# An attention and expert block on one core: the shared up weights of the tail fetched once, its first rows fetched early

## Chip, core and metric

The kernel runs on one core of one Trainium2 chip. The metric is the device time of one execution in microseconds, as the median of several runs. The profile is one further execution, recorded by the hardware profiler; its times are counted from the start of its span.

The engines are named as in the profile: PE (TensorE, matmuls; PEld its weight loads), DVE (VectorE), ACT (ScalarE), POOL (GpSimd), SP (SyncE, which here only issues transfers). "SPq", "ACTq" and "POOLq" are the queues of these engines where they issue a DMA.

## The reference

Eight sequences of 512 tokens with 512 features go through an attention block and a block of experts, each between two layer norms and with a residual. All is in float32.

```python
x = L0_attn_x                                   # 8 x 512 x 512
x = x + layernorm(attention(layernorm(x)))      # 16 heads, latent projections, rope scores
h = layernorm(x)
scores = sigmoid(h @ router_weight.T)           # 16 experts, 2 chosen per token, in groups
routed = sum over the 2 chosen: weight * relu2(h @ w_up[e]) @ w_down[e]     # 512 -> 256 -> 512
shared = relu2(h @ shared_up) @ shared_down                                 # 512 -> 1024 -> 512
x = x + layernorm(routed + shared)
```

`relu2` is the square of the ReLU. The shared part is computed for every token, the routed part only for the two experts of each token.

## The kernel before

There are four stages.

1. **Attention, with a side list.** A loop runs over the eight batches and 16 steps per batch. Beside the scores of a batch stand the closing work of the batch before (output projection, norm, router, scatter of its rows to `table`, sorted by expert) and, as fill, the shared part of earlier batches. `shared_list` (L641) makes that fill: per half batch (256 tokens, `a` = 0, 1) eight up chunks and four down pieces. The shared part is done here for all but the last `LATE = 2` batches, and its rows are stored to `s_rows` in DRAM. The rows after attention are stored to `x_rows` (L439).
2. **plan()** (L653) works out which tile of 128 routed rows belongs to which expert.
3. **routed()** (L728) runs over `NTILES` = 79 tiles of 128 rows: `fetch_rows` (L738) loads rows from `table`, `fetch_weights` (L743) loads one expert's up and down weights (512 KB each) into one of three sets if the expert has changed, `turn`, `up` and `down` compute, and ACT stores each result to `y_rows` (L789). In the loop at L797 tile j is computed, then SP issues the rows of tile j + 3 and the weights of tile j + 2.
4. **The tail** (L963 to L987) does the shared part of the last two batches and completes all 32 token tiles. `prepare` (L811) takes a slot of the pool `end`, loads the tile's `x_rows` and, for an early tile, its `s_rows` (256 KB each, on SP), and lets POOL gather the tile's two routed rows from `y_rows` (two indirect DMAs of 128 rows, L817). `complete` (L827) adds the parts on DVE (L830, L834), takes the norm's statistics (L213 to L217, L839), scales on ACT (L842), adds the residual on POOL (L843), and puts the store to `out` (L847) on a list. The list is emptied in the next `complete`.

The 24 tiles of the first six batches are early tiles: their shared rows come from `s_rows`. The eight tiles of the last two batches are late: their shared part comes straight from PSUM. The list `items` (L966 to L978) puts one early tile behind every two up chunks and one behind each late tile. So each half of a late batch completes eight tiles, in the order early, early, early, early, late, early, late, early; with four halves that makes 32.

In the tail the program's order is kept on PE and SP as written. DVE, ACT and POOL get theirs from a scheduler, and each works in order. SP's queue is one list: a store that waits for POOL's addition holds back all loads and weight fetches behind it. `LEAD = 6` tiles are prepared ahead, then tile n + 6 when tile n is completed. With `SLOTS = 10` slots a load of tile n waits until tile n - 10 is stored.

The up weights of the shared part (512 x 1024, 2 MB) come in pieces of 256 columns (512 KB) with two buffers. `load_wsu` (L590) is called by the first chunk of each piece and fetches that piece and the next:

```python
        if (b, a, i) not in wsu_ and b < B:
            wsu = sh.tile([P, NK, INTER], F32, tag="wsu", name=f"wsu_{b}_{a}_{i}", bufs=2)
            cols = shared_up[:, i * P : i * P + INTER]
            nc.sync.dma_start(wsu, cols.rearrange("(c p) i -> p c i", p=P))
```

A half batch uses four pieces, the tail 16. `shared_up_chunk` (L597) runs four matmuls per chunk (L609), then ReLU on ACT (L616) and the square on DVE (L617). `shared_down_tile` (L619) runs the down product (L624), 16 matmuls for one tile of 128 tokens in two pieces.

Of the kernel before, what the change touches and what calls it, by code (L numbers as in the profile page):

```python
# [11 lines left out]
F32 = mybir.dt.float32  # L12
# [5 lines left out]
P = 128  # L18
# [20 lines left out]
def sandwich_kernel(  # L39
# [28 lines left out]
    nc = tc.nc  # L68

    B, S, D = x.shape  # L70
    NE, _, INTER = w_up.shape
    HID = shared_up.shape[1]
    NT = S // P
    NK = D // P
    NI = INTER // P
    NH = HID // P
# [10 lines left out]
    ps_s = ctx.enter_context(tc.tile_pool(name="ps_s", bufs=2, space=PSUM))  # L87
    ps_o = ctx.enter_context(tc.tile_pool(name="ps_o", bufs=4, space=PSUM))
    dram = ctx.enter_context(tc.tile_pool(name="dram", bufs=1, space=bass.MemoryType.DRAM))
    until_tail = ExitStack()  # L90
    sb = until_tail.enter_context(tc.tile_pool(name="sb", bufs=1))
    until_routed = ExitStack()
    at = until_routed.enter_context(tc.tile_pool(name="at", bufs=1))

# [2 lines left out]
    NTILES = (TOP_K * T) // P + NE - 1  # L97
# [6 lines left out]
    def load_rows(src, b, name):  # L104
        t = sh.tile([P, NT, D], F32, tag="x", name=f"{name}_{b}", bufs=2)
        for i in range(NT):
            nc.sync.dma_start(t[:, i, :], src[b, i * P : (i + 1) * P, :])
        return t
# [304 lines left out]
    ao, xT, sc_, comb_, chosen_, slot_ = {}, {}, {}, {}, {}, {}  # L413

    def project_out(b, i):
        if i == 0:
            ao[b] = sb.tile([P, NT, D], F32, tag="ao", name=f"ao_{b}")
            res[b] = load_rows(x, b, "res")
        ps = ps_o.tile([P, D], F32, tag="o", name=f"ps_ao_{b}_{i}")
        for c in range(NK):  # L420
            nc.tensor.matmul(  # L421
                ps,
                lhsT=ctxs[b, c][:, i * P : (i + 1) * P],
                rhs=wo[:, c, :],
                start=(c == 0),
                stop=(c == NK - 1),
            )
        nc.vector.tensor_tensor(ao[b][:, i, :], ps, bo, ALU.add)
# [159 lines left out]
    hT, wsu_, ysum = {}, {}, {}  # L588

    def load_wsu(b, a, i):  # L590
        if (b, a, i) not in wsu_ and b < B:
            wsu = sh.tile([P, NK, INTER], F32, tag="wsu", name=f"wsu_{b}_{a}_{i}", bufs=2)
            cols = shared_up[:, i * P : i * P + INTER]
            nc.sync.dma_start(wsu, cols.rearrange("(c p) i -> p c i", p=P))
            wsu_[b, a, i] = wsu

    def shared_up_chunk(b, a, i, late):  # L597

        if i % NI == 0:
            load_wsu(b, a, i)  # L600
            load_wsu(b + (a and i + NI == NH), a ^ (i + NI == NH), (i + NI) % NH)
        if i == 0:
            hT[b] = sh.tile([P, NH, HALF], F32, tag="hT", name=f"hT_{b}_{a}")
        if late:
            ps = ps_s.tile([P, 2, S], F32, tag="s", name=f"h_{b}_{a}_{i}")[:, 0, :]
        else:
            ps = ps_o.tile([P, S], F32, tag="o", name=f"h_{b}_{a}_{i}")
        for k in range(NK):
            nc.tensor.matmul(  # L609
                ps[:, 0:HALF],  # L610
                lhsT=wsu_[b, a, i - i % NI][:, k, (i % NI) * P : (i % NI + 1) * P],
                rhs=xT[b][:, k, a * HALF : (a + 1) * HALF],
                start=(k == 0),
                stop=(k == NK - 1),
            )
        nc.scalar.activation(hT[b][:, i, :], ps[:, 0:HALF], AF.Relu)  # L616
        nc.vector.tensor_tensor(hT[b][:, i, :], hT[b][:, i, :], hT[b][:, i, :], ALU.mult)  # L617
# [21 lines left out]
    UP, DOWN = 1.72, 3.43  # L639

    def shared_list(b, finish, late=False):  # L641
        got = []
        for a in range(2):
            got += [(UP, lambda a=a, i=i: shared_up_chunk(b, a, i, late)) for i in range(NH)]
            got += [
                (DOWN, lambda a=a, t=t, i=i: shared_down_tile(b, a, t, i, finish))
                for t in range(NT // 2)
                for i in range(2)
            ]
        return got  # L650
# [77 lines left out]
    def routed(rt, lists):  # L728
# [14 lines left out]
        def fetch_weights(j):  # L743
            e = nc.sync.value_load(lists[0:1, 1, j : j + 1], min_val=0, max_val=NE - 1)
            load = nc.sync.value_load(lists[0:1, 2, j : j + 1], min_val=0, max_val=1)
            wu, wd = sets[j % NBUF]
            nc.sync.dma_start(
                wu, w_up[bass.ds(e, 1)].rearrange("o (c p) i -> p (o c) i", p=P), cond=load
            )
            nc.sync.dma_start(  # L750
                wd, w_down[bass.ds(e, 1)].rearrange("o (c p) d -> p (o c) d", p=P), cond=load
            )
# [44 lines left out]
        for j in range(NTILES + 1):  # L797
            if j + 1 < NTILES:
                turn(j + 1)
            if j < NTILES:  # L800
                up(j)
            if j > 0:
                down(j - 1)
            if j + AHEAD < NTILES:
                fetch_rows(j + AHEAD)
            if j + NBUF - 1 < NTILES:
                fetch_weights(j + NBUF - 1)

    def prepare(c, with_shared):  # L811
        t = end.tile([P, 4, D], F32, tag="end", name=f"end_{c}", bufs=SLOTS)
        nc.sync.dma_start(t[:, 0, :], x_rows[c * P : (c + 1) * P, :])
        if with_shared:
            nc.sync.dma_start(t[:, 1, :], s_rows[c * P : (c + 1) * P, :])
        for j in range(TOP_K):
            nc.gpsimd.indirect_dma_start(  # L817
                out=t[:, 2 + j, :],
                out_offset=None,
                in_=y_rows[:, :],  # L820
                in_offset=bass.IndirectOffsetOnAxis(ap=back[:, c, j : j + 1], axis=0),
            )
        return t

    SLOTS, LEAD = 10, 6

    def complete(c, t, shared=None):  # L827

        acc = t[:, 1, :]
        nc.vector.scalar_tensor_tensor(  # L830
            acc, t[:, 2, :], weight[:, c, 0:1], acc if shared is None else shared,
            ALU.mult, ALU.add,
        )
        nc.vector.scalar_tensor_tensor(  # L834
            acc, t[:, 3, :], weight[:, c, 1:2], acc, ALU.mult, ALU.add
        )
        mv, rstd = norm_stats([acc], f"y{c}")
        off = small.tile([P, 1], F32, tag="off", name=f"off_{c}")
        nc.vector.scalar_tensor_tensor(  # L839
            off, mv[:, 0, 0:1], -1.0, rstd, ALU.mult, ALU.mult  # L840
        )
        nc.scalar.activation(acc, acc, AF.Identity, bias=off, scale=rstd)  # L842
        nc.gpsimd.tensor_tensor(acc, acc, t[:, 0, :], ALU.add)  # L843
        while stores:
            stores.pop()()
        b, i = divmod(c, NT)
        stores.append(lambda: nc.sync.dma_start(out[b, i * P : (i + 1) * P, :], acc))  # L847

    stores = []


    LATE = 2
# [103 lines left out]
            f()  # L956
    until_routed.close()
    lists = plan()
    rt = until_tail.enter_context(tc.tile_pool(name="rt", bufs=1))
    with tc.manual_schedule(engines={mybir.EngineType.PE, mybir.EngineType.SP}):  # L960
        routed(rt, lists)
    until_tail.close()
    end = ctx.enter_context(tc.tile_pool(name="end", bufs=1))  # L963
    with tc.manual_schedule(engines={mybir.EngineType.PE, mybir.EngineType.SP}):

        early, items, ups, downs = iter(range((B - LATE) * NT)), [], 0, 0  # L966
        for b in range(B - LATE, B):
            late = iter(range(b * NT, (b + 1) * NT))
            for cost, f in shared_list(b, lambda ps, c: complete(c, ready.pop(c), ps), True):
                ups += cost == UP  # L970
                downs += cost == DOWN
                done = cost == DOWN and downs % 2 == 0
                items.append((f, next(late) if done else None))
                if done or cost == UP and ups % 2 == 0:
                    c = next(early, None)
                    if c is not None:
                        items.append((lambda c=c: complete(c, ready.pop(c)), c))
        items += [(lambda c=c: complete(c, ready.pop(c)), c) for c in early]  # L978
        order = [c for _, c in items if c is not None]
        ready = {}  # L980
        for f, c in [(None, None)] * LEAD + items:
            if f is not None:
                f()
            if (f is None or c is not None) and order:
                n = order.pop(0)
                ready[n] = prepare(n, n < (B - LATE) * NT)
        stores.pop()()  # L987


# [35 lines left out]
```

## Time and profile before

| what | value |
|---|---|
| three runs, median (lowest to highest) | 1939.24 us (1935.95 to 1941.33) |
| profiled execution, whole | 1946.77 us |
| profiled execution, span | 1945.1 us |
| mean granted clock of TensorE in it | 0.942 |
| busy: PE / DVE / ACT / POOL | 1726.6 / 1033.1 / 893.3 / 577.7 us |
| last routed product on PE (L780) begins | 1741.84 us |
| first and last gather on POOL (L817) begin | 1751.9 and 1908.0 us |
| last addition on POOL (L843) begins | 1940.5 us |
| transfers from 1735 to 1945 us | 48.91 MB |
| the same, by kind | 32 x_rows, 24 s_rows, 64 gathers, 32 stores (256 KB each), 15 up-weight pieces (512 KB each) |

The page gives an engine's busy time as a mean over the whole span. The tail is only a tenth of it, so it has to be read from the views that can be cut to a stretch of time: the timeline of one engine, and the busy times by window. In a line of a timeline the first number is the start, the second the duration, both in us; the bracket at the end gives the idle time before it and what ended that. "PEclk" is the share of TensorE's full clock that was granted, "DMA share" the mean busy share of the core's 16 DMA engines; small overlaps can take it a little above 1.

### The profile page before, as it was taken

How to read it: one execution, taken by the hardware profiler on the slowest of the kernel's cores; microseconds unless marked ns; L12 is line 12 of the kernel's file. 1: busy time of each engine (PE TensorE's matmuls, PEld its weight loads, DVE VectorE, ACT ScalarE, POOL GpSimd, SP SyncE). 2: the span in 40 equal slices, each digit the busy share in tenths (PEclk: the TensorE clock that was granted, in tenths of full speed). 3: DMA queues.
4: the chain of work that ended last, by engine and by line, in shares of the span. 5: the costliest groups of instructions: out<-in, count | busy, mean ns of one | idle time of the engine just before them, and what ended most of it. 6: DMA issues, size and time to landing. Idle time of an engine off the chain costs nothing. (4 is left out here: it accounts for less than half of the span.)

```text
span 1945.1 us, 27230 instructions
## 1 busy us (share of the span) xinstructions
PE 1726.6 (89%) x8968; PEld 1044.0 (54%) x8968; DVE 1033.1 (53%) x2695; ACT 893.3 (46%) x1977; POOL 577.7 (30%) x714
## 2 busy tenths in 40 slices
PE   7898999999999999999999989889689999996665
PEld 3444645555555545554655544445366777764443
DVE  4667745664665475446745665754522222225674
ACT  4866654654555555455545656751022222221222
POOL 1433332342324232423422353451100000006563
PEclk9999999999989998999999899889889999997787
DMA  6001111130112111211310110012456465578774
GB/s 199 1 23 44 63 58 44 55 109 33 45 54 93 49 50 39 82 49 55 105 36 23 55 66 1 22 44 70 179 184 233 131 207 180 196 266 283 261 267 153
DMA packets 125901, 199.62 MB, mean 103 GB/s; under 512 B 14145, under 2 KB 60225, under 8 KB 125761
## 3 DMA queue, kind: packets, MB, share of 16 engines
q1 hardware_dynamic: 102992, 141.50, 21.6%
q0 software_dynamic: 10240, 33.56, 4.6%
q10 hardware_dynamic: 12528, 22.81, 3.7%
q8 instruction: 73, 1.20, 0.2%
q14 instruction: 68, 0.55, 0.1%
HBM read 190.50 MB, written 65.01 MB: 131 GB/s over the span
## 5 line engine op out<-in xcount | busy, mean ns | idle before, releaser
L389 POOL TENSOR_SCALAR p<-p,rden 128x512 f32<-128x512 f32 x512 | 362.3, 726 | 788.6 <-DVE rden L387 480.7
L355 ACT ACTIVATE p<-p,nmax 128x512 f32<-128x512 f32 x512 | 363.8, 712 | 168.9 <-DVE nmax L345 161.6
L345 DVE CUSTOM_DVE_ANT_0 p<-s,rope 128x512 f32<-128x512 f32 x512 | 326.2, 686 | 93.1 <-PE s L333 69.0
L375 PEld LDWEIGHTS pt<-ident,p 128*128 128x128 f32 x2048 | 237.3, 146 | 183.7 <-issue 132.7
L609 PE MATMUL h<-xT,wsu 128*128 128x256 f32 x1024 | 251.0, 405 | 79.4 <-DMA wsu<-in_L_ffn_shared_up_dram 49.3
L375 PE MATMUL pt<-ident,p 128*128 128x128 f32 x2048 | 287.8, 285 | 25.4 <-DVE pT L378 9.1
L378 DVE COPY pT<-pt 128x512 f32<-128x512 f32 x256 | 175.1, 686 | 203.9 <-PE pt L375 197.7
L609 PEld LDWEIGHTS h<-xT,wsu 128*128 128x128 f32 x1024 | 206.2, 205 | 125.9 <-issue 50.8
L624 PE MATMUL y<-wsd,hT 128*128 128x512 f32 x512 | 228.5, 597 | 3.5 <-DVE pT L378 3.5
L380 ACT COPY pT<-pt 128x512 f32<-128x512 f32 x256 | 146.3, 576 | 112.2 <-PE pt L375 111.6
L817 POOL DMA_INDIRECT end<-y_rows,back x64 | 66.0, 1031 | 372.3 <-DMA end<-x_rows 354.3
L765 PE MATMUL hg<-xgT,set_up 128*128 128x128 f32 x1264 | 158.5, 280 | 13.3 <-DMA set_up<-in_L_ffn_w_up_dram 12.5
L333 PE MATMUL s<-k,q 32*128 32x512 f32 x1024 | 162.0, 671 | 1.9 <-DVE nmax L345 1.8
L624 PEld LDWEIGHTS y<-wsd,hT 128*128 128x128 f32 x512 | 96.6, 192 | 120.6 <-issue 111.0
L765 PEld LDWEIGHTS hg<-xgT,set_up 128*128 128x128 f32 x1264 | 150.8, 196 | 15.9 <-issue 11.8
L402 PE MATMUL o<-pT,v 128*32 128x512 f32 x1024 | 139.9, 625 | 18.7 <-DVE pT L378 17.9
L780 PE MATMUL yg<-set_down,hgT 128*128 128x512 f32 x316 | 149.7, 597 | 0.0
L774 DVE TENSOR_TENSOR hgT<-hgT 128x256 f32<-128x256 f32 x79 | 33.6, 426 | 186.4 <-ACT hgT L773 186.4
L617 DVE TENSOR_TENSOR hT<-hT 128x256 f32<-128x256 f32 x128 | 60.8, 477 | 122.4 <-ACT hT L616 117.3
L759 ACT COPY xgT<-pt_g 128x512 f32<-128x512 f32 x79 | 46.3, 586 | 161.8 <-PE pt_g L757 161.7
L616 ACT ACTIVATE hT<-h 128x256 f32<-128x256 f32 x128 | 48.5, 382 | 155.7 <-PE h L609 146.6
L421 PE MATMUL ps_ao<-wo,ctx 128*128 128x512 f32 x256 | 112.5, 593 | 0.0
(163 smaller groups left out, 1837.1 us busy)
## 6 DMA issues: line engine op xcount, KB each, us to landing
set_up<-in_L_ffn_w_up_dram SPq DMA_DIRECT2D x79, 512.0 KB
set_down<-in_L_ffn_w_down_dram SPq DMA_DIRECT2D x79, 512.0 KB
wsu<-in_L_ffn_shared_up_dram SPq DMA_DIRECT2D x64, 512.0 KB
xg<-table SPq DMA_DIRECT2D x79, 256.0 KB
y_rows<-ysb ACTq DMA_DIRECT2D x79, 256.0 KB
x<-in_L_attn_x_dram SPq DMA_DIRECT2D x32, 256.0 KB
res<-in_L_attn_x_dram SPq DMA_DIRECT2D x32, 256.0 KB
x_rows<-res SPq DMA_DIRECT2D x32, 256.0 KB
```

Of the source, the lines that this page charges most:

```text
L333: nc.tensor.matmul(tiles[-1][:, h % 2, :], lhsT=q[r0 : r0 + HEAD_DIM, qt * P : (qt + 1) * P], rhs=k[r0 : r0 + HEAD_DIM, :], start=True, st ...
L345: nc.vector.tensor_tensor_reduce(out=pr[:, h, :], in0=tiles[h // 2][:, h % 2, :], in1=rope[b, qt], scale=-1.0, scalar=3.0e38, op0=ALU.add, ...
L355: nc.scalar.activation(pr[:, h, :], pr[:, h, :], AF.Exp, bias=nmax[:, h : h + 1], scale=-1.0, accum_out=den[:, h : h + 1],)
L375: nc.tensor.transpose(pt[:, c, :], pr[:, h, c * P : (c + 1) * P], ident)
L378: nc.vector.tensor_copy(to, pt)
L380: nc.scalar.copy(to, pt)
L389: nc.gpsimd.tensor_scalar(pr[:, h, :], pr[:, h, :], rden[:, h : h + 1], 1.0, ALU.mult, ALU.mult)
L402: nc.tensor.matmul(ps[r0 : r0 + HEAD_DIM, :], lhsT=vs[b][:, c, col : col + HEAD_DIM], rhs=pT[:, h, c, :], start=(c == 0), stop=(c == NT - 1),)
L609: nc.tensor.matmul(ps[:, 0:HALF], lhsT=wsu_[b, a, i - i % NI][:, k, (i % NI) * P : (i % NI + 1) * P], rhs=xT[b][:, k, a * HALF : (a + 1) * ...
L624: nc.tensor.matmul(ysum[c], lhsT=hT[b][:, i, t * P : (t + 1) * P], rhs=wsd[:, i, :], start=(i == 0), stop=(i == NH - 1),)
L765: nc.tensor.matmul(ph[:, 0, i * P : (i + 1) * P], lhsT=sets[j % NBUF][0][:, k, i * P : (i + 1) * P], rhs=xgT[j][:, k, :], start=(k == 0), ...
L780: nc.tensor.matmul(py, lhsT=hg[j][:, i * P : (i + 1) * P], rhs=sets[j % NBUF][1][:, i, :], start=(i == 0), stop=(i == NI - 1),)
```

## The change

- The up weights of the late batches are no longer fetched in pieces. A tile `wsu_all` of 2 MB holds all of `shared_up`; it is fetched once, from inside `routed()`, behind the weights fetched in iteration j = 39. Its pool `late` is taken behind attention, in the space that attention's tiles leave.
- `prepare` is split into `load_end` (row loads on SP) and `gather_end` (gathers on POOL). The loads of the first `EARLY = 4` tiles stand at the end of the routed stage; their slots lie in the pool `late`.
- There are nine slots for ten (four in `late`, five in `end`), the lead is five tiles for six, and a store is issued when two tiles more have been completed (`LAG = 2`), not one.
- `ao` moves from the pool `sb` to the pool `at`, which ends before `plan()`; `sb` stays to the end.

```diff
-    until_tail = ExitStack()
-    sb = until_tail.enter_context(tc.tile_pool(name="sb", bufs=1))
+    sb = ctx.enter_context(tc.tile_pool(name="sb", bufs=1))
...
-            ao[b] = sb.tile([P, NT, D], F32, tag="ao", name=f"ao_{b}")
+            ao[b] = at.tile([P, NT, D], F32, tag="ao", name=f"ao_{b}")
...
-        if (b, a, i) not in wsu_ and b < B:
+        if (b, a, i) not in wsu_ and b < B - LATE:
...
-        if i % NI == 0:
-            load_wsu(b, a, i)
-            load_wsu(b + (a and i + NI == NH), a ^ (i + NI == NH), (i + NI) % NH)
+        if late:
+            wsu = wsu_all[:, :, i * P : (i + 1) * P]
+        else:
+            if i % NI == 0:
+                load_wsu(b, a, i)
+                load_wsu(b + (a and i + NI == NH), a ^ (i + NI == NH), (i + NI) % NH)
+            wsu = wsu_[b, a, i - i % NI][:, :, (i % NI) * P : (i % NI + 1) * P]
...
-                lhsT=wsu_[b, a, i - i % NI][:, k, (i % NI) * P : (i % NI + 1) * P],
+                lhsT=wsu[:, k, :],
...
+            if j == NTILES // 2:
+                nc.sync.dma_start(wsu_all, shared_up.rearrange("(c p) n -> p c n", p=P))
...
-    def prepare(c, with_shared):
-        t = end.tile([P, 4, D], F32, tag="end", name=f"end_{c}", bufs=SLOTS)
+    SLOTS, EARLY, LEAD, LAG = 9, 4, 5, 2
...
+    def load_end(n, c, with_shared):
+
+        pool, k = (late, EARLY) if n % SLOTS < EARLY else (end, SLOTS - EARLY)
+        t = pool.tile([P, 4, D], F32, tag="end", name=f"end_{c}", bufs=k)
         nc.sync.dma_start(t[:, 0, :], x_rows[c * P : (c + 1) * P, :])
         if with_shared:
             nc.sync.dma_start(t[:, 1, :], s_rows[c * P : (c + 1) * P, :])
+        return t
+
+    def gather_end(c, t):
         for j in range(TOP_K):
...
-    SLOTS, LEAD = 10, 6
...
-        while stores:
-            stores.pop()()
+        while len(stores) > LAG - 1:
+            stores.pop(0)()
...
+    late = ctx.enter_context(tc.tile_pool(name="late", bufs=1))
+    wsu_all = late.tile([P, NK, HID], F32, name="wsu_all")
+    until_tail = ExitStack()
     rt = until_tail.enter_context(tc.tile_pool(name="rt", bufs=1))
     with tc.manual_schedule(engines={mybir.EngineType.PE, mybir.EngineType.SP}):
         routed(rt, lists)
+        for n, c in enumerate(order[:EARLY]):
+            ready[c] = load_end(n, c, c < (B - LATE) * NT)
     until_tail.close()
...
-            if (f is None or c is not None) and order:
-                n = order.pop(0)
-                ready[n] = prepare(n, n < (B - LATE) * NT)
-        stores.pop()()
+            if (f is None or c is not None) and n < len(order):
+                c = order[n]
+                if n >= EARLY:
+                    ready[c] = load_end(n, c, c < (B - LATE) * NT)
+                gather_end(c, ready[c])
+                n += 1
+        for f in stores:
+            f()
```

The lists `items` and `order` are built as before, only ahead of the routed stage.

More of the change, by code (lines that the diff above doesn't have):

```diff
@@ L807, in routed @@
                 fetch_weights(j + NBUF - 1)
-    def prepare(c, with_shared):
-        t = end.tile([P, 4, D], F32, tag="end", name=f"end_{c}", bufs=SLOTS)
+            if j == NTILES // 2:
+                nc.sync.dma_start(wsu_all, shared_up.rearrange("(c p) n -> p c n", p=P))
+    SLOTS, EARLY, LEAD, LAG = 9, 4, 5, 2
+    slots_end = []
+    def load_end(n, c, with_shared):
+        pool, k = (late, EARLY) if n % SLOTS < EARLY else (end, SLOTS - EARLY)
+        t = pool.tile([P, 4, D], F32, tag="end", name=f"end_{c}", bufs=k)
         nc.sync.dma_start(t[:, 0, :], x_rows[c * P : (c + 1) * P, :])
@@ L822, in prepare @@
             )
-        return t
-    SLOTS, LEAD = 10, 6
     def complete(c, t, shared=None):
@@ L958, in sandwich_kernel @@
     lists = plan()
+    early, items, ups, downs = iter(range((B - LATE) * NT)), [], 0, 0
+    for b in range(B - LATE, B):
+        last = iter(range(b * NT, (b + 1) * NT))
+        for cost, f in shared_list(b, lambda ps, c: complete(c, ready.pop(c), ps), True):
+            ups += cost == UP
+            downs += cost == DOWN
+            done = cost == DOWN and downs % 2 == 0
+            items.append((f, next(last) if done else None))
+            if done or cost == UP and ups % 2 == 0:
+                c = next(early, None)
+                if c is not None:
+                    items.append((lambda c=c: complete(c, ready.pop(c)), c))
+    items += [(lambda c=c: complete(c, ready.pop(c)), c) for c in early]
+    order = [c for _, c in items if c is not None]
+    ready = {}
+    late = ctx.enter_context(tc.tile_pool(name="late", bufs=1))
+    wsu_all = late.tile([P, NK, HID], F32, name="wsu_all")
+    until_tail = ExitStack()
     rt = until_tail.enter_context(tc.tile_pool(name="rt", bufs=1))
@@ L964, in sandwich_kernel @@
     with tc.manual_schedule(engines={mybir.EngineType.PE, mybir.EngineType.SP}):
[L966 to L980, printed above, removed]
+        n = 0
         for f, c in [(None, None)] * LEAD + items:
```

## The prediction

> **What bounds the kernel now.** I began with the page's picture of the span in 40 slices.
>
> ```profile
> PE   7898999999999999999999989889689999996665
> PEclk9999999999989998999999899889889999997787
> DMA  6001111130112111211310110012456465578774
> GB/s 199 1 23 44 63 58 44 55 109 33 45 54 93 49 50 39 82 49 55 105 36 23 55 66 1 22 44 70 179 184 233 131 207 180 196 266 283 261 267 153
> ```
>
> TensorE carries the kernel until the last four slices. There its share falls to 5 or 6 tenths while the DMA engines are at their busiest. The timeline of PE puts the last routed product at 1745 us, so the tail is 200 us. It runs in four equal phases, each half of a late batch: eight up chunks, four down pieces, eight finished tiles (six early, two late). POOL's timeline marks them: L843 (the last addition of a tile) resumes after a long wait when the phase's first late tile is ready.
>
> ```profile
> 1797.79 2.94 POOL L843 TENSOR_TENSOR end<-end 128x512 f32<-128x512 f32 x2 [10.14 <-ACT end L842]
> ...
> 1843.81 2.49 POOL L843 TENSOR_TENSOR end<-end 128x512 f32<-128x512 f32 x2 [13.97 <-ACT end L842]
> ...
> 1889.48 2.94 POOL L843 TENSOR_TENSOR end<-end 128x512 f32<-128x512 f32 x2 [13.06 <-ACT end L842]
> ...
> 1932.38 2.49 POOL L843 TENSOR_TENSOR end<-end 128x512 f32<-128x512 f32 x2 [22.14 <-ACT end L842]
> ```
>
> The first gather starts at 1751.93, so the tail is 45.9 + 46.0 + 45.7 + 55.6 us (the last from 1889.48 to the end at 1945.1). The view of busy times in these stretches (elapsed, then PE, PEld, DVE, ACT, POOL, clock, DMA share, GB/s) shows no engine full:
>
> ```profile
> 1751.90:1797.80 45.90, 32.76 (x96) 21.25 (x96) 26.20 (x51) 7.62 (x18) 29.21 (x29) 0.78 0.82 288
> 1797.80:1843.80 46.00, 27.68 (x78) 17.88 (x78) 29.11 (x55) 10.91 (x25) 26.63 (x24) 0.78 0.76 263
> 1843.80:1889.50 45.70, 33.60 (x111) 21.98 (x110) 29.67 (x58) 11.09 (x25) 27.30 (x25) 0.89 0.74 264
> 1889.50:1932.40 42.90, 26.20 (x83) 17.01 (x82) 24.51 (x49) 10.94 (x25) 18.70 (x17) 0.80 0.53 185
> ```
>
> So a loop of waits sets each phase. PE's timeline shows one arm: the third chunk waits for an up-weight piece (15.78 us in phase 2, and in phase 4:)
>
> ```profile
> 1906.88 9.55 PE L609 MATMUL h<-xT,wsu 128*128 128x256 f32 x32 [16.04 <-DMA wsu<-in_L_ffn_shared_up_dram]
> ...
> 1920.62 13.90 PE L624 MATMUL y<-wsd,hT 128*128 128x512 f32 x32
> ```
>
> That piece is issued late because SyncE's queue holds it behind stores. The table of SyncE's own waits (total us, times, longest) for the tail:
>
> ```profile
> SPq L847 <- POOL end L843: 100.2, 17, 18.6
> SPq L594 <- PE h L609: 23.7, 6, 6.7
> ```
>
> The other arm is the rows of a phase's last early tiles. SyncE issued the second of the loads below at 1872.25; VectorE got its rows at 1883.34, 11 us later, since the DMA share was 1.0 from 1868 to 1880.
>
> ```profile
> 1881.54 0.75 DVE L830 SCALAR_TENSOR_TENSOR end<-end,weight 128x512 f32<-128x512 f32 x1 [6.85 <-DMA end<-s_rows]
> ...
> 1883.34 0.75 DVE L830 SCALAR_TENSOR_TENSOR end<-end,weight 128x512 f32<-128x512 f32 x1 [0.26 <-DMA end<-s_rows]
> ```
>
> VectorE works in order. The late tile's sum stands behind these rows, so they, not PE's product (ready at 1880.5), set 1889.48. In the last phase no rows are left and PE's arm sets the end.
>
> [...] rows from SyncE are late while POOL's gathers fill the engines at 375 to 410 GB/s. [...] PEclk is 0.50 in 1804 to 1816 [...], and an up matmul takes up to 796 ns against 378 at least.
>
> **The change part by part.**
>
> *Bytes.* One tile's 128 rows are 0.262 MB. A phase moves 8 x_rows, 6 s_rows, 16 gathers and 8 stores, 38 x 0.262 = 9.96 MB, and four up pieces of 0.524, together 12.06 MB; over 46 us that is 262 GB/s, as the windows say. The change takes the 2.1 MB away (15 fetches in the tail), and in the first phase also eight row loads, 2.1 MB, which go behind the last weight fetch of the routed stage (1736 to 1742, DMA share 0.18), so they cost nothing.
>
> *Routed stage.* In their place one fetch of 2.1 MB goes into SyncE's queue after the weights of tile 41, at 1579. In before this spot is followed by six weight pairs from 1581.63 on, and PE already stalls once:
>
> ```profile
> 1593.49 3.00 PE L765 MATMUL hg<-xgT,set_up 128*128 128x128 f32 x16 [2.74 <-DMA set_up<-in_L_ffn_w_up_dram]
> ```
>
> At 375 GB/s the fetch takes 5.6 us. The pair for tile 42 then lands near 1588.3 + latency against its use at 1586.64: about 2.5 us of stall; the next is pushed by some 1.5 us more, net of the idle DMA share (0.2 to 0.3 over 10 us). PE has no slack in this stage, so I take +4.0, between 0 (absorbed) and +8 (2.1 MB at the 274 GB/s seen there). ACT's y_rows store of tile 39 to 40 may queue behind it too; that lies within these ends.
>
> *First gather.* The last y_rows store is issued at 1746.20 and shared the engines with eleven row loads; now with four. I take -1.5 (0 to -2.5).
>
> *Phase 1.* Its gathers are paced by POOL: 24 gathers of 1.25 us and four additions end 35.7 us after the first (1787.65). The new order lets the first late tile wait for tile 10, two gathers earlier: 35.7 - 2.5 [...], then product-sum 0.75, offset 0.2, ACT 0.8 and gaps 0.1 give 37.8. Bytes to that point are about 10.0 MB, or 262 GB/s, below the 375 it can do. -8.1.
>
> *Phases 2 and 3.* POOL's 16 gathers and 8 additions took 32.1 and 32.6 us from the phase's start; the last early tile needed is two gathers earlier, so 30.0. [...] From the second product-sum of that tile to POOL's addition: 1884.13 to 1889.48 less the late tile's first sum (0.75), which the new order puts ahead, 4.6. Sum 37.2, so -8.8 and -8.5. Bounds: 35 if POOL's order runs unhindered, 41 if gathers land 6 us late, since 9.96 MB in 32 us is 311 GB/s, near what the engines do. PE is not late: chunk 5's ReLU stands behind ACT's tile 11 (about +18), two chunks, then 7 us for the first down tile, +28; it is needed at +34.
>
> *Last phase.* Tile 27's activation ends at 1907.09, +17.6; chunk 7 of 1.8 us (3.1 at half clock), ReLU and square put the downs near +20.5 in place of +31.1; the second late tile's product is done 13.9 later, and from there to the end it is 10.6 as now (1934.52 to 1945.1). 45.0 for 55.6: -10.6.
>
> *Slots 9 for 10, lead 5 for 6, stores two behind.* In SyncE's order a load of tile n+7 still follows the store of tile n, as before, but it now waits for store n-2 of the same nine slots to land, where it waited for n-3. Stores come 2.5 us or more apart on average, two of them cover a landing of 5 us: 0, up to +1 a phase. POOL's first new gathers (tiles 14, 15) wait likewise; 0.
>
> Sum: +4.0 - 1.5 - 8.1 - 8.8 - 8.5 - 10.6 = -33.5. The profiled execution took 1946.77 (span 1945.1), 7.5 above the median of 1939.24; the saving is taken from the median: **1905.7 us**.
>
> **Rivals.** *Landings stay late.* Share 1.0 stretches speak for it, the fewer bytes against. If the last gather lands 8 us after issue, phases 1 to 3 are 43.2, 42.6 and 42.6 long: -2.7 - 3.4 - 3.1 - 10.6 - 1.5 + 4 = -17.3, so 1921.9. *POOL becomes the bound and never waits:* 64 x 1.25 + 32 x 1.42 = 125.4 us after the first gather, plus 3.4 to the end: -1.5 + 4 against 193.2 - 128.8, so -61.9, 1877.3. It needs late tiles that never wait for their rows; the order against it. *Slower:* the ring of slots takes over. With two stores per landing a tile takes half a landing; at 5.75 us a tile now, it decides from landings of 11.5 us. Rows did take 11 us under load. At 13 us the 23 reusing tiles take 150 us against 132: +17.5, and +4 from the routed stage, 1960.7. Against it: the long landings came with the bytes that go. That the fetches don't move is excluded by the order of instructions: 16 pieces are gone, one large fetch stands in the routed stage.
>
> **How the numbers follow.** Forecast 0.71, late landings 0.18, POOL bound 0.05, slot ring 0.06. Bounds low: routed 0, gather -2.5, phases 35 (35.5 in the first): -45, 1894, and 2 more if the last phase runs at full clock. High: routed +8, phases 41, last 48: about -15, 1924, which takes in the rival of late landings. Range 1892 to 1924. Below 0.3% (6 us) this measurement can't tell a change. Faster 0.91; same 0.03, the slot ring's weak side; slower 0.06.
>
> **What would show it.** Right: no wait for up weights in the tail's PE timeline; L843's long waits some 37 us apart; tail 158 us from first gather; a new stall of 2 to 5 us at set_up near 1587. Wrong: the wait for s_rows before the late tile's sum persists, SyncE waits at L823 for out_dram stores, or the routed stage grows by more than 8 us.

## The result and the profile after

The changed kernel took 1913.52 us, median of four runs (1911.08 to 1921.25), against 1939.25 us of the kernel before in the same job. The ratio is 0.9876, with a 95% interval of 0.9844 to 0.9907: faster, by 25.7 us. The profiled execution took 1911.08 us, its span 1909.4.

The page's picture in 40 slices of the changed kernel, to be laid beside that of before:

```profile
PE   6999999999999999999999989979959998999686
PEclk9999899999999999999999989999979999999889
DMA  6000121131023101211121110012176548477884
GB/s 202 10 14 34 48 85 45 56 111 34 23 67 104 45 34 50 95 50 51 39 89 45 56 67 1 22 45 66 61 249 198 165 137 287 136 271 241 278 279 160
```

PE's last four slices read 9, 6, 8, 6 where they were 6, 6, 6, 5: the tail is shorter (166.5 us from its first chunk to the end, before 199.8) and PE is busier in it. POOL's timeline gives the same four marks (the residual addition is L853 now):

```profile
1791.22 2.94 POOL L853 TENSOR_TENSOR end<-end 128x512 f32<-128x512 f32 x2 [3.54 <-ACT end L852]
...
1829.57 2.94 POOL L853 TENSOR_TENSOR end<-end 128x512 f32<-128x512 f32 x2 [7.55 <-ACT end L852]
...
1866.98 2.94 POOL L853 TENSOR_TENSOR end<-end 128x512 f32<-128x512 f32 x2 [6.16 <-ACT end L852]
...
1896.73 2.49 POOL L853 TENSOR_TENSOR end<-end 128x512 f32<-128x512 f32 x2 [9.12 <-ACT end L852]
```

The first gather starts at 1750.42. So the phases are 40.8, 38.35, 37.4 and 42.4 us long, where they were 45.9, 46.0, 45.7 and 55.6. The waits ahead of these additions, 10 to 22 us before, are 3.5 to 9: POOL has less idle time left. The busy times by stretch (elapsed, then PE, PEld, DVE, ACT, POOL, clock, DMA share, GB/s):

```profile
1750.40:1791.20 40.80, 25.67 (x79) 15.46 (x77) 26.04 (x50) 8.34 (x18) 30.75 (x28) 0.86 0.73 232
1791.20:1829.60 38.40, 31.02 (x96) 19.29 (x96) 26.88 (x58) 10.43 (x25) 26.75 (x25) 0.93 0.76 260
1829.60:1867.00 37.40, 31.93 (x93) 19.71 (x94) 30.21 (x57) 10.24 (x25) 26.77 (x25) 0.86 0.79 266
```

In PE's timeline of the tail no wait names up weights any more; before, seven waits for pieces came to 46.9 us. What is left is waits for ScalarE's ReLU, 32.3 us in all:

```profile
1792.17 9.58 PE L612 MATMUL h<-xT,wsu_all 128*128 128x256 f32 x32 [12.81 <-ACT hT L619]
...
1846.37 3.78 PE L612 MATMUL h<-xT,wsu_all 128*128 128x256 f32 x8 [4.50 <-ACT hT L619]
```

SyncE's own waits in the tail (total us, times, longest) show the queue still standing behind stores, 123.2 us in all, but nothing urgent stands there now. The last line is the whole of what loads waited for slots:

```profile
SPq L857 <- POOL end L853: 123.2, 26, 22.2
...
SPq L823 <- DMA out_dram<-end: 0.7, 1, 0.7
```

The other arm of the prediction was the rows ahead of a late tile's sum. In the kernel before, VectorE's last wait for a transfer ahead of each of the first three marks named the shared rows (`s_rows`, ended at 1791.69, 1837.67 and 1883.34). In the changed kernel these waits (ended at 1783.14, 1823.67 and 1860.42) name gathered rows; the first and the third of them:

```profile
1783.14 0.75 DVE L844 SCALAR_TENSOR_TENSOR end<-end,weight 128x512 f32<-128x512 f32 x1 [1.30 <-DMA end<-y_rows,back]
...
1860.42 0.75 DVE L844 SCALAR_TENSOR_TENSOR end<-end,weight 128x512 f32<-128x512 f32 x1 [0.53 <-DMA end<-y_rows,back]
```

So the shared rows set no mark any more. What VectorE waits for last is what POOL fetches.

**Where the time went, stage by stage, in the two profiled executions.** From the first routed product to the tail's first chunk 327.97 became 334.22 us (+6.25). From there to the first gather 6.65 became 7.47 (+0.8). The phases gave -5.1, -7.7, -8.3 and -13.2. Sum, before rounding: -27.1. The spans differ by 35.7. The other 8.6 us lie ahead of the first routed product, which began at 1408.73 in place of 1417.31. That is scatter between executions: in the traces below it begins between 1412 and 1418 us, and at 1415.99 when the changed kernel ran again. So -27.1 stands beside the -25.7 of the medians.

### The profile page after: what moved, and what is told of

Same layout as the page of the kernel before. It is cut to its first block, busy times and chain, and to the rows that moved or that the text cites. A ratio compares the mean times of both kernels' runs of the same rounds, so it can differ in the third digit from the quotient of the medians.

```text
span 1909.4 us, 27180 instructions
## 1 busy us (share of the span) xinstructions
PE 1718.2 (90%) x8968; PEld 1036.8 (54%) x8968; DVE 1027.8 (54%) x2695; ACT 892.1 (47%) x1977; POOL 578.8 (30%) x714
## 4 chain that ended last, share of the span: by engine, by line
PE 59%; DVE 16%; issue 6%; DMA 6%; POOL 6%; ACT 4%; SPq 2%; POOLq 0%; DVEq 0%
PE pt L374 8%; PE y L627 7%; PE h L612 7%; PE hg L768 6%; DVE p L344 6%; PE yg L783 6%; PE o L401 6%; PE s L332 5%; PE ps_ao L420 4%; ACT p L354 3%; DMA set_up<-in_L_ffn_w_up_dram 2%; DVE pT L377 2%; POOL end L830 2%; POOL p L388 2%; PE ps_r L477 2%
## 5 line engine op out<-in xcount | busy, mean ns | idle before, releaser
L612 PE MATMUL h<-xT,wsu 128*128 128x256 f32 x768 | 175.9, 387 | 15.3 <-DVE pT L377 12.5
L768 PE MATMUL hg<-xgT,set_up 128*128 128x128 f32 x1264 | 160.7, 282 | 13.4 <-DMA set_up<-in_L_ffn_w_up_dram 13.2
L612 PEld LDWEIGHTS h<-xT,wsu 128*128 128x128 f32 x768 | 146.4, 194 | 45.5 <-DVE pT L377 21.1
```

The lines of the kernel that those rows point to most:

```text
L612: nc.tensor.matmul(ps[:, 0:HALF], lhsT=wsu[:, k, :], rhs=xT[b][:, k, a * HALF : (a + 1) * HALF], start=(k == 0), stop=(k == NK - 1),)
L768: nc.tensor.matmul(ph[:, 0, i * P : (i + 1) * P], lhsT=sets[j % NBUF][0][:, k, i * P : (i + 1) * P], rhs=xgT[j][:, k, :], start=(k == 0), ...
```

## The experiments

Times are medians, and each job ran the kernel before beside its kernels. Its median was 1941.1 us in the first job (the next four experiments), 1944.6 in the second (changed kernel again, `e7`, `e8`, `e9`) and 1940.0 in the third (`e10` to `e13`); comparisons across jobs are made by ratios. The stage lengths come from each kernel's own trace, by the same marks as above.

**1. The fetch in another place (e1_quiet).** Behind the weights of tile 27, where no expert begins.

```diff
-            if j == NTILES // 2:
+            if j == 25:
```

> The one large fetch of up weights is issued at routed tile 25, in a stretch without weight loads (DMA share 0.33 to 0.54), and not at tile 39, just ahead of six weight pairs. My theory: the routed stage, 334.2 us from its first up product to the tail's first chunk in the changed kernel's trace against 328.0 before, falls back to 328 to 330, the tail stays 166 us, and the median falls from 1913.5 to 1908 to 1910. Rival (the 6.2 us are scatter between executions, or come from another part): no wait for xg or set_up near the fetch goes away, routed stays above 333, median within 2 us of 1913.5.

Measured: 1913.33 us, ratio 0.9854 (0.9833 to 0.9875). The routed stage took 329.1 us in place of 334.2. One stall on rows stayed, at the new place (PE's timeline of this kernel):

```profile
1528.48 0.63 PE L760 MATMUL pt_g<-ident,xg 128*128 128x128 f32 x4 [2.70 <-DMA xg<-table]
1528.94 3.13 PE L768 MATMUL hg<-xgT,set_up 128*128 128x128 f32 x16
```

The sixteen products after the stall took 3.13 us, those of the tiles around it 1.95. The forecast for the routed stage came true, the one for the median (1908 to 1910) did not: the ratio doesn't tell the gain of the routed stage from nothing. This trace's last phase was 46.4 us long, but the unchanged "after" varies almost as far (42.4, and 45.6 when it ran again), so a loss in the tail isn't shown.

**2. No early rows (e2_noearly).**

```diff
-    SLOTS, EARLY, LEAD, LAG = 9, 4, 5, 2
+    SLOTS, EARLY, LEAD, LAG = 9, 0, 5, 2
```

> The first four tiles' rows are loaded at the tail's start with the others (no early loads), all else as in the changed kernel. My theory: 2.1 MB come back into phase 1, the first gather starts up to 1 us later and phase 1 is 2 to 5 us longer (43 to 46 for 40.8), phases 2 to 4 stay at 38, 37, 42; median 1916 to 1919. Rival (the early rows make most of the gain): the tail grows by 12 us or more, median above 1925.

Measured: 1916.49 us, ratio 0.9869 (0.9847 to 0.9891), not told from the ratio with them. The first phase took 40.2 us, not longer than 40.8, and the first gather came 6.7 us after the tail's first chunk in place of 7.5. The expected lengthening did not come: the 2.1 MB of early rows are not what limits the first phase.

**3. Weights in pieces again, all else as changed (e3_pieces).** `load_wsu` and its pieces in the tail as before; nine slots, lead 5, four early tiles, stores two behind.

```diff
-        if late:
-            wsu = wsu_all[:, :, i * P : (i + 1) * P]
-        else:
-            if i % NI == 0:
+        if i % NI == 0:
...
-            if j == NTILES // 2:
-                nc.sync.dma_start(wsu_all, shared_up.rearrange("(c p) n -> p c n", p=P))
```

> The up weights come in pieces again as before; early rows, nine slots, lead 5 and stores two behind stay. My theory (the pieces' bytes and PE's wait for them set the old phases): phases 2 and 3 return to 44 to 47 us and the last to 53 to 56, phase 1 keeps 3 to 5 us, no stall is added in the routed stage; median 1931 to 1937. Rival (early rows and the freer queue of stores make the gain): phases 2 and 3 at 40 or less, median below 1922.

Measured: 1925.51 us, ratio 0.992 (0.9895 to 0.9946), between what the theories said: the rest of the change is worth 15.6 us without resident weights. Phases of 39.6, 43.4, 44.3 and 50.3; PE waits for pieces again, 16.22 us in the second.

**4. Resident weights alone (e6_resident).** Slots, lead, store order and row loads as before.

```diff
-    SLOTS, EARLY, LEAD, LAG = 9, 4, 5, 2
+    SLOTS, EARLY, LEAD, LAG = 10, 0, 6, 1
```

> Only the resident up weights: fetched once at routed tile 39, but ten slots, lead 6, no early rows and stores one behind, as before. My theory: nearly all of the gain is here: phase 1 43 to 46, phases 2 and 3 37 to 39, last 42 to 45; routed stage + 6; median 1915 to 1920. Rival (nine slots with stores two behind matter): phases 2 and 3 at 42 or more, median above 1925.

Measured: 1915.54 us, ratio 0.9848 (0.9822 to 0.9873): the whole gain. The first phase took 41.2 us, less than the 43 to 46 expected, though no rows came early; the last took 44.0. POOL's marks:

```profile
1794.65 2.94 POOL L853 TENSOR_TENSOR end<-end 128x512 f32<-128x512 f32 x2 [3.54 <-ACT end L852]
1832.19 2.94 POOL L853 TENSOR_TENSOR end<-end 128x512 f32<-128x512 f32 x2 [6.17 <-ACT end L852]
1869.77 2.95 POOL L853 TENSOR_TENSOR end<-end 128x512 f32<-128x512 f32 x2 [6.99 <-ACT end L852]
```

Phases 2 and 3 are 37.5 and 37.6 us with lead 6. So one part of the prediction's reason for them, that the new order makes the last early tile's gathers come two gathers earlier, isn't needed: with lead 6 they are just as short.

Taken together, experiments 3 and 4 show that the way the weights come is the cause of the gain: with it alone the whole gain is there, without it 10 us of it are missing. They don't separate its two effects, that the pieces no longer come late and that each phase moves 2.1 MB less.

**What holds a phase at 37 us?** In the changed kernel's trace one stretch of phase 3 shows it. VectorE, POOL and ScalarE, each from its own timeline:

```profile
1839.88 5.27 DVE L849 SCALAR_TENSOR_TENSOR off<-mv_y,rstd_y 128x1 f32<-128x1 f32 x1
```

```profile
1840.21 4.91 POOL L853 TENSOR_TENSOR end<-end 128x512 f32<-128x512 f32 x4
1845.28 0.96 POOL L830 DMA_INDIRECT end<-y_rows,back  x1 [0.16 <-DVE off L849]
```

```profile
1845.23 0.81 ACT L852 ACTIVATE end<-end,off,rstd_y 128x512 f32<-128x512 f32 x1 [4.90 <-DVE off L849]
1845.95 0.64 ACT L619 ACTIVATE hT<-h 128x256 f32<-128x256 f32 x2
```

One VectorE operation on 128 x 1 numbers, 0.16 us elsewhere, took 5.27 us: it ended when POOL's four additions in a row (4.91 us) ended. ScalarE's scaling waited 4.90 us for it, the ReLUs of two chunks stood behind that scaling, and the 4.50 us of PE at 1846.37, shown above, are the wait for those ReLUs. The small operation was held through four instructions of POOL, not one. What in the hardware holds it isn't shown. By the recorded starts it even began 0.33 us ahead of the first of them, and still did not get through. In the same tail five calls of L849 touch an addition; they took 1.35 to 5.27 us, and each ended within 0.03 us of an addition's end. The 17 that ran beside a gather alone took at most 0.23. So POOL's additions cost twice, in POOL's own time (16 gathers and 8 additions fill 27 of 37 us, 31 with the gaps of 0.30 us behind each gather) and in VectorE's. The next runs test whether they hold the tail.

**5. The changed kernel again (after_again)**, to stand beside the next three.

> The changed kernel once more, to stand beside the next three on one chip. 1910 to 1917 us by every theory; routed stage near 334 us, phases near 40, 38, 37.5 and 42.5.

Measured: 1917.78 us (1908.81 to 1925.88), ratio 0.9871 (0.984 to 0.9901). Routed stage 331.5, first gather after 7.2, phases 41.2, 37.7, 37.4, 45.6.

**6. The residual addition on VectorE (e7_dveadd).**

```diff
-        nc.gpsimd.tensor_tensor(acc, acc, t[:, 0, :], ALU.add)
+        nc.vector.tensor_tensor(acc, acc, t[:, 0, :], ALU.add)
```

> The residual addition of a finished tile (L853) on VectorE in place of POOL. Theory 1, POOL's additions are what is left: in the changed kernel a 128x1 operation of VectorE that takes 0.16 us alone took 5.27 us while four additions of POOL (4.91 us) ran, ScalarE and PE waited behind it (4.90 and 4.50 us), and POOL's 16 gathers and 8 additions fill 31 of a phase's 37.5 us. Without them a phase takes 32 to 34 us, no VectorE operation is stretched to several us, and the run comes to 1897 to 1904 us. Theory 2, VectorE or the landings set the phase: VectorE gets 8 x 0.75 = 6 us more in each phase, the phases stay at 37 to 40 us and the run at 1911 to 1920 us.

Measured: 1899.09 us, ratio 0.978 (0.9754 to 0.9806), 18.7 us below the changed kernel beside it. Theory 1 holds. The view of the operation's durations (count, then min/median/max in ns), in the changed kernel:

```profile
L849 DVE SCALAR_TENSOR_TENSOR off<-mv_y,rstd_y x30: 141/158/5268, 1761.2 to 1895.9; 128x1 f32<-128x1 f32 x30
```

and with the additions on VectorE:

```profile
L849 DVE SCALAR_TENSOR_TENSOR off<-mv_y,rstd_y x32: 142/156/161, 1766.9 to 1892.4; 128x1 f32<-128x1 f32 x32
```

No call of it is stretched any more. The phases of 32.6 and 33.5 us are as theory 1 put them; the first, at 36.8, is longer. The stretches of this kernel, cut at the same addition:

```profile
1756.00:1792.80 36.80, 25.98 (x75) 15.37 (x73) 23.11 (x53) 8.91 (x17) 27.32 (x26) 0.87 0.80 265
1792.80:1825.40 32.60, 30.01 (x96) 19.28 (x96) 25.59 (x65) 10.08 (x25) 18.20 (x16) 0.93 0.92 315
1825.40:1858.90 33.50, 30.67 (x96) 19.71 (x96) 26.04 (x65) 10.69 (x26) 16.03 (x16) 0.90 0.87 297
1858.90:1898.40 39.50, 26.31 (x80) 16.17 (x80) 28.32 (x72) 13.35 (x29) 5.87 (x6) 0.88 0.50 174
```

VectorE got eight operations more per phase, at 0.69 us each, and yet was busy for less: 25.6 and 26.0 us in phases 2 and 3 against 26.9 and 30.2. Its busy time in the changed kernel was partly waiting. The edit takes away both costs of POOL's additions at once, their time on POOL (busy 18.2 and 16.0 us in phases 2 and 3, against 26.8 in the changed kernel) and VectorE's waiting; how the 18.7 us divide between them isn't shown. What fills these phases now is PE with 30 us and the DMA engines with a share of 0.87 to 0.92.

**7. The fetch in four pieces (e8_split)**, each 256 columns, in iterations 20, 22, 24 and 26 (`QUIET`).

```diff
-            if j == NTILES // 2:
-                nc.sync.dma_start(wsu_all, shared_up.rearrange("(c p) n -> p c n", p=P))
+            if j in QUIET:
+                q = slice(QUIET.index(j) * INTER, QUIET.index(j) * INTER + INTER)
+                nc.sync.dma_start(
+                    wsu_all[:, :, q], shared_up[:, q].rearrange("(c p) n -> p c n", p=P)
+                )
```

> The fetch of the shared up weights in four pieces of 0.5 MB, behind the weights of tiles 22, 24, 26 and 28, where no expert begins. Theory 1, the fetch cost what PE waited for: the stalls on rows (2.55 us) and on expert weights behind it (2.26 us and less) go, and the slow products after them; the routed stage takes 325 to 329 us in place of 334, and the run 1905 to 1909 us. Theory 2, the gain is given back in the tail, as the single fetch in a quiet place did (its last phase was 4 us longer): 1911 to 1915 us with the routed stage just as short.

Measured: 1910.01 us (1904.58 to 1922.48), ratio 0.9836 (0.9804 to 0.9869), against 0.9871 beside it. The routed stage took 325.8 us, and no stall on rows is left in it, so its part of theory 1 holds. The median is 7.8 us lower, just short of the expected, and the two intervals overlap: the gain in the whole time is likely, not shown.

Over all traces the routed stage tells the cost of the fetch. With one fetch at tile 39: 334.2, 333.9, 334.3, 331.5, 332.1 us, mean 333.2. With none (before, `e3`, `e10`, `e11`, `e13`): 328.0, 323.3, 324.5, 328.1, 324.9, mean 325.8. The fetch in one piece at that place cost 7.4 us; in four pieces (325.8, 326.7, 321.7) it cost nothing that can be seen. The four pieces also stand at another place, so part of this is the place: in one piece at tile 25 (`e1_quiet`, a single trace) the stage took 329.1. Four pieces at tile 39 were not tried.

**8. Both (e9_both).**

> The additions on VectorE and the fetch in four pieces together. If both theories 1 hold and the two gains lie on the same path one after the other, they add up: 1890 to 1897 us. If only the additions count: 1897 to 1904. If neither: 1911 or more.

Measured: 1897.23 us (1895.1 to 1899.87), ratio 0.9767 (0.9742 to 0.9793), the lowest ratio of all, just outside what was expected if both count. It beats both kernels, the changed one by 20.6 us. Against the additions alone (1899.09) the split isn't told from nothing.

**9. Stores two behind, alone (e10_lag).** The kernel before, with its pieces, ten slots and lead 6. It is built from the changed kernel (`e3_pieces` with `SLOTS, EARLY, LEAD, LAG = 10, 0, 6, 2`); against the kernel before, this is what acts in the tail:

```diff
-        while stores:
-            stores.pop()()
+        while len(stores) > LAG - 1:
+            stores.pop(0)()
```

> The kernel before with one thing changed: stores two tiles behind (ten slots, lead 6, no early rows, up weights in pieces as before). Theory 1, the pieces of up weights were late because SyncE's queue held them behind a store that waits for POOL, so a store one tile later lets them go: phases 2 and 3 of 42 to 44 us in place of 46.0 and 45.7, 1923 to 1931 us. Theory 2, the gain without resident weights came from the early rows or the shorter lead: 1937 to 1944 us.

Measured: 1932.74 us, ratio 0.9963 (0.9948 to 0.9979), 7.2 us faster. Phases 2 and 3 took 43.0 and 42.1 us as theory 1 said, the first 47.1. The gain was a little smaller than forecast (1931 at most). The queue did hold pieces behind stores, but one tile more of freedom frees only part: PE still waits for them, 12.55 and 12.59 us in phases 2 and 4 where it was 15.78 and 16.04.

```profile
1806.97 9.45 PE L609 MATMUL h<-xT,wsu 128*128 128x256 f32 x32 [12.55 <-DMA wsu<-in_L_ffn_shared_up_dram]
...
1893.02 7.19 PE L609 MATMUL h<-xT,wsu 128*128 128x256 f32 x24 [12.59 <-DMA wsu<-in_L_ffn_shared_up_dram]
```

**10. Early rows, alone (e11_early).** The kernel before with four early tiles of ten.

```diff
-    SLOTS, EARLY, LEAD, LAG = 9, 4, 5, 2
+    SLOTS, EARLY, LEAD, LAG = 10, 4, 6, 1
```

(to `e3_pieces`.)

> The kernel before with one other thing changed: the rows of the first four tiles fetched inside the routed stage (ten slots, lead 6, stores one tile behind, up weights in pieces). Theory 1 (the stores): nothing of weight, 1936 to 1944 us, the first phase 44 to 47 us. Theory 2 (the early rows): 1923 to 1931 us, the first phase near 41 us and the later ones as before.

Measured: 1945.25 us, ratio 1.0027 (1.0015 to 1.0038): a little slower. Phases 46.2, 47.1, 46.5, 55.8. Seven of the eight early loads are issued from 1732.77 to 1737.27, inside the routed stage. The eighth, and every load behind it, waits in SyncE's queue for a store of `y_rows` to land, until 1743.19:

```profile
SPq L820 <- DMA y_rows<-ysb: 5.5, 1, 5.5
```

and the first gather starts 7.8 us after the tail's first chunk. In nine traces with early rows this takes 7.3 us on average, in five without 6.3. That is 1.2 us of the loss of 5.3 (6.65 became 7.8); the phases are each up to 1 us longer as well, and no run gives the cause.

The stores (-7.2) and the early rows (+5.3) do not add up to the -15.6 of `e3_pieces`. Its first phase is 39.6 us, against 47.1 and 46.2 here, and PE waits only 3.51 and 2.22 us for pieces there. Whether that is the shorter lead with its nine slots by itself, or only together with the stores, was not tried apart.

**11. A tenth slot in the best version (e12_slots10)**, lead 6.

> The additions on VectorE and the fetch in four pieces, and a tenth slot with lead 6. If rows wait for free slots (nine slots, stores two behind), the phases of 32.6 and 33.4 us shorten by 1 to 3 us each and the run takes 1888 to 1893 us. If slots don't count: 1894 to 1900 us.

Measured: 1896.72 us, ratio 0.9781 (0.9754 to 0.9808), against 0.9767 with nine. A tenth slot with lead 6 brings nothing that can be seen.

**12. The kernel before with the additions on VectorE (e13_before_dve).**

> The kernel before with the residual additions on VectorE and nothing else. If POOL's additions became a bound only once the up weights no longer came late: 1934 to 1944 us. If they held the tail back just as much before: 18 us less, 1922 to 1927 us, with phases of 41 to 42 us.

Measured: 1934.73 us, ratio 0.9964 (0.9948 to 0.998), 5.3 us faster, against 18.7 us for the same edit in the changed kernel. So in the kernel before the additions were hidden for the most part. The waits for pieces, which stay, are the likely reason (PE's timeline of this kernel):

```profile
1810.11 9.42 PE L609 MATMUL h<-xT,wsu 128*128 128x256 f32 x32 [10.88 <-DMA wsu<-in_L_ffn_shared_up_dram]
...
1855.24 9.04 PE L609 MATMUL h<-xT,wsu 128*128 128x256 f32 x32 [11.12 <-DMA wsu<-in_L_ffn_shared_up_dram]
```

## Why the prediction was right, and where its sum was off

Forecast 1905.7 us in a range of 1892 to 1924; measured 1913.52. The mechanism held in the main: PE's waits for late pieces went (46.9 us to none), the shared rows no longer come last ahead of a late tile's sum, and the resident weights alone give the whole gain (`e6_resident`, where the last rows are gathered ones too). Of the signs named beforehand, PE waits for no up weights, POOL's marks stand 37 to 38 us apart in phases 2 and 3, the tail takes 159.0 us from the first gather where 158 was forecast, and a stall of 2.26 us at `set_up` is there at 1585. Of the signs of being wrong only a trace is there: SyncE waits once at L823 for a store, 0.7 us. The change saved 25.7 us where the sum said 33.5. Term by term, in the profiled executions:

| step | predicted | measured |
|---|---|---|
| routed stage | +4.0 | +6.25 |
| first gather | -1.5 | +0.8 |
| phase 1 | -8.1 | -5.1 |
| phase 2 | -8.8 | -7.7 |
| phase 3 | -8.5 | -8.3 |
| last phase | -10.6 | -13.2 |
| sum | -33.5 | -27.1 |

- **Routed stage.** The stall was put at tile 42's weights near 1587 and bounded by 0 and 8 us; over five traces against five it measured 7.4, so +4.0 was too small. The term left out the rows in the same queue. SyncE's and PE's timelines of the changed kernel, around the fetch (`wsu_all`):

```profile
1572.18 0.40 SPq L812 DMA_DIRECT2D wsu_all<-in_L_ffn_shared_up_dram  x1
1573.36 0.34 SPq L744 DMA_DIRECT2D xg<-table  x1
1580.40 0.39 SPq L750 DMA_DIRECT2D set_up<-in_L_ffn_w_up_dram  x1
```

```profile
1582.47 0.63 PE L760 MATMUL pt_g<-ident,xg 128*128 128x128 f32 x4 [2.55 <-DMA xg<-table]
1585.36 3.55 PE L768 MATMUL hg<-xgT,set_up 128*128 128x128 f32 x16 [2.26 <-DMA set_up<-in_L_ffn_w_up_dram]
```

  The rows issued 1.2 us behind the fetch reached PE 9.1 us later, and the next weights were issued only at 1580.40. So PE stood twice, 2.55 and 2.26 us, and the sixteen products that followed took 3.55 us where they take 1.95. PE's granted clock was 0.50 from 1585.16 on for 3.41 us. The stretch came behind stops of 2.55 and 2.26 us, and the prediction's term held nothing for a lower clock.
- **First gather.** The saving from fewer row loads did not come. That the early loads "cost nothing" was wrong too: the last of them waits in SyncE's queue for a `y_rows` store (4.4 us in the changed kernel, 5.5 in `e11_early`), and the loads behind it with it. The sign was wrong, and the term off by 2.3 us.
- **Phases 1 to 3.** 37.8, 37.2 and 37.2 were forecast, 40.8, 38.35 and 37.4 measured. The sizes are near, the reasons only partly right, and that they come so near is in part luck. How long a gather takes to land, which the sums needed, was not shown by the trace of before. In the changed kernel the median is 4.9 us (the last number of the line, from the DMA view of the tail):

```profile
end<-x_rows SPq DMA_DIRECT2D x31, 256.0 KB, 4.6
...
end<-y_rows,back POOLq DMA_INDIRECT x64, 4.9
```

  With these 4.9 us the sum for phases 2 and 3 would be 39.5 (30.0 + 4.9 + 4.6). The two gathers saved by the new order are not seen (`e6_resident`), and phase 1 is as short without early rows (40.2, `e2_noearly`). And what POOL's additions do to VectorE was in no term. It was visible before the change: in the tail of before the same small operation reached 3732 ns against a median of 156.

```profile
L839 DVE SCALAR_TENSOR_TENSOR off<-mv_y,rstd_y x32: 130/156/3732, 1765.3 to 1938.4; 128x1 f32<-128x1 f32 x32
```

- **Readings.** From 1868 to 1880 us POOL's gathers did not fill the DMA engines by themselves: they moved 1.90 of 4.60 MB, SyncE's own transfers 2.70. And in phase 3 of the kernel before PE's long wait (11.38 us) was ended by ScalarE's scaling, not by a piece; there the prediction let the rows set the phase.
- **Last phase.** PE's downs began at 1884.98, 18.0 us after the phase's start, where +20.5 was forecast: 42.4 us for 45.0. When the same kernel ran again it took 45.6, so this term is within its scatter.
- **The rivals.** The slot ring did not take over (0.7 us of waiting for slots, and a tenth slot brings nothing). Late landings took a part, with 4.9 us, not 8. "POOL becomes the bound" was priced as POOL never waiting and given 0.05. What happened lies between: POOL still waits 3.5 to 9 us a phase, but its additions hold VectorE, ScalarE and PE. Taking them off POOL moves 18.7 us.

## What to carry to other kernels

When a wait is removed, look in the trace of before for an operation whose longest duration is far above its median. Here it pointed to the next bound, POOL's additions, worth 5.3 us before the change and 18.7 after it. Data that many stages use in pieces can be fetched once ahead of them, but mind where and how large: 2 MB at once, ahead of six weight pairs, cost 7 us of a stage that PE fills, four times 0.5 MB in a stretch without weight loads nothing that could be seen. Of a change with several parts, run each alone: here one part gave the whole gain, another by itself 7 us, a third by itself a loss, and the gains did not add up.

## What the runs showed of the hardware

- In the changed kernel a VectorE operation on 128 x 1 numbers (L849) ended only when a whole row of POOL additions had ended, not one: it took 5.27 us beside four (4.91 us), 0.16 us without. Beside POOL's gathers alone it was not held (at most 0.23 us). An addition of 128 x 512 takes 0.69 us on VectorE and 1.27 us on POOL (medians).
- "Busy" of VectorE includes such waiting: with 32 additions of 0.69 us more, 22 us of work, it was busy for 103.1 us after the first gather in place of 107.7.
- A short stop of PE cost more than itself: in the kernel before, after 2.74 us without work, PE's granted clock was 0.50 for 3.41 us from 1594.32 on, and sixteen products took 3.00 us in place of 1.95. In the routed stages of the two profiled executions of before and after, behind the first products, the stops of 1.94, 2.28, 2.38 and 2.74 us and the pair of 2.55 and 2.26 us were each followed by such a stretch; those of 1.41, 1.56 and 2.47 us were not.
